# Count matrices from groups of 2 nodes with one tile of 128 edges each, and 18 instead of 16 dense blocks in attention 1

## The chip, the cores and the metric

The kernel runs on one core of one Trainium2 chip. The metric is the device time of one execution in microseconds. Of the core's engines, PE is the matrix engine (PEld its weight loads), DVE the vector engine, ACT the scalar engine, POOL the engine that issues the gathers here, and SP a queue for transfers.

## The reference

Two graph layers over 6250 nodes of 128 features and 200,000 edges (`src`, `dst`), which come sorted by `dst`. What matters here is the first, a graph attention in two layers, the first with 4 heads of 16 features and the second with one head:

```python
feat = (x @ W).reshape(num_nodes, H, D)
el = jnp.sum(feat * attn_l[None], axis=-1)
er = jnp.sum(feat * attn_r[None], axis=-1)
e = jax.nn.leaky_relu(el[src] + er[dst], NEG_SLOPE)
m = jax.ops.segment_max(e, dst, num_segments=num_nodes)
ee = jnp.exp(e - m[dst])
s = jax.ops.segment_sum(ee, dst, num_segments=num_nodes)
msg = feat[src] * (ee / s[dst])[:, :, None]
rst = jax.ops.segment_sum(msg, dst, num_segments=num_nodes)
```

The second graph layer is a convolution: a small network on each edge's attributes gives weights, the source node's row is gathered and combined with them, and the results are summed by `dst`.

## The kernel before

The nodes form 49 blocks of 128 (`NB`). The program has four stages, one after the other.

*Preparation.* `src` and `dst` are loaded and put into 16-bit integers (`raw`). The rows of x are normalised, multiplied by W1 and written to `table1`, 76 values a node. For counting, each group of W = 8 neighbouring destination nodes needs the place of its first edge in the sorted list: `belowc`, `wbelow` and `wseg` (L587 to L594) find the segment of 160 edges by comparing, seven gathers (L597) fetch those segments, and L601 to L608 make `wfirst` from them. A group starts anywhere, so its edges are read from the next lower multiple of WSTEP = 32, as a run of WCAP = 384 edges.

*Attention 1.* There are two ways to treat a block of destination nodes. An **edge block** (33 of them, `NG = NB - DENSE1`) goes over its up to 34 × 128 edges: POOL gathers a row of `table1` for each edge (L306, 34 indirect transfers a block, in groups of 8), DVE makes a one-hot matrix of destinations (`ohr`, L315) and the messages, PE sums them (`whole`, L362). The groups share 6 gather buffers `G`. A **dense block** (16, in pairs, `dense1`) uses no edges but a count matrix: how many edges go from each source node to each destination node. For 7 source blocks at a time and each head, ACT makes 7 `ramp` tiles (L833), DVE takes the minimum with the counts (`up`, L835), PE multiplies with `rc` (L847), a table of source rows that SP loads one step ahead. `ramp` and `up` have two buffers each. At a pair's end `finish1` writes its results.

The count matrices of all 49 blocks are made within attention 1 too, since attention 2 runs on them alone. `write_runs` writes `runs`, an array in device memory that has the 384 edges from each multiple of 32, during the first 4 edge blocks. `cut_windows` fetches the runs of 128 groups (16 groups are a block of nodes, so 7 such chunks), makes a `key` (source block × 8 + place in the group, with a large number added where the edge isn't of the group) and `lo` (place in the source block), and turns both with PE (`lot`, `keyt`). `count` then takes two groups: DVE compares `lot` with 0..127 (`lo`, L723) and `keyt` with 392 slots (`key`, L726), three tiles of 128 edges each; PE multiplies the two one-hot matrices, six matmuls of 392 columns (L731), three a group; ACT copies the sums to `ca` (L732), and ACT's queue writes a quarter of a block's counts to device memory (L922). Both comparisons read their constant side from a PSUM tile (`slots`).

The order of work is written in one loop over the edge blocks. After each group of gathers it adds count steps and dense steps in proportion, by two due counts: count steps from block LAG = 5, dense steps from block LAG_D = 8. From this program a scheduler makes the order within each engine; each engine then works in order.

*Attention 2* uses the count matrices for all 49 blocks, with the same sort of ramps and minima. *The convolution* gathers again, 34 transfers a block over all 49.

Of the kernel before, what the change touches and what calls it, by code (L numbers as in the profile page):

```python
# [26 lines left out]
F32 = mybir.dt.float32  # L27
# [11 lines left out]
P = 128  # L39
# [4 lines left out]
W, T = 8, 3  # L44
WCAP = P * T
WSEG = 160
WSTEP = 32
HS = 7
LAG = 5
AHEAD = 4  # L50
DENSE1, LAG_D = 16, 8
# [10 lines left out]
def gnn_kernel(ctx: ExitStack, tc: tile.TileContext, x, src, dst, attr4, attr8,  # L62
# [23 lines left out]
    assert WB % (2 * NQ) == 0  # L86
# [149 lines left out]
    raws = []  # L236
    for t in both:
        raw = pool.tile([P, ROWT + WCAP], BF16, tag="row", name="raw", bufs=2)[:GP].bitcast(I16)
        nc.scalar.copy(raw, t)
        raws.append(raw)  # L240
# [297 lines left out]
    slot_k = pool.tile([P, NKEY, 2], BF16, name="slot_k")  # L538
    nc.gpsimd.iota(slot_k, pattern=[[1, NKEY], [0, 2]], base=-(NKEY // 2), channel_multiplier=0,
# [9 lines left out]
    for b0 in range(0, NB, 4):  # L549
# [9 lines left out]
        for j in range(len(bs)):  # L559
# [18 lines left out]
    wstarts = find.tile([GP, NC * P], F32, name="wstarts")  # L578
    nc.gpsimd.iota(wstarts, pattern=[[W, NC * P]], base=0, channel_multiplier=0,
                   allow_small_or_imprecise_dtypes=True)  # L580
    NS = ROWT // WSEG
    wbelow = find.tile([GP, NC * P], F32, name="wbelow")
    ps = small()
    for c in range(NC):
        cs = slice(c * P, (c + 1) * P)
        below = find.tile([GP, P, NS], F32, name="belowc")
        nc.vector.tensor_tensor(below, df[:, 0:ROWT:WSEG][:, None, :].to_broadcast([GP, P, NS]),  # L587
                                wstarts[:, cs, None].to_broadcast([GP, P, NS]), op=OP.is_lt)
        nc.vector.tensor_reduce(wbelow[:, cs], below, axis=AX.X, op=OP.add)
        nc.tensor.matmul(ps[:, c:c + 1], wbelow[:, cs], ones[:GP], start=True, stop=True)  # L590
    wseg = find.tile([P, NC], F32, name="wseg")
    nc.vector.tensor_scalar(wseg, ps[:, :NC], -1.0, 0.0, op0=OP.add, op1=OP.max)
    wseg_i = find.tile([P, NC], I32, name="wseg_i")
    nc.vector.tensor_copy(wseg_i, wseg)  # L594
    wpart_i = find.tile([P, NC, WSEG], I32, name="wpart_i")
    for c in range(NC):
        nc.gpsimd.indirect_dma_start(  # L597
            out=wpart_i[:, c, :], out_offset=None, in_=dst.rearrange("(s t) -> s t", t=WSEG),
            in_offset=bass.IndirectOffsetOnAxis(ap=wseg_i[:, c:c + 1], axis=0))
    wpart = find.tile([P, NC, WSEG], F32, name="wpart")  # L600
    nc.vector.tensor_copy(wpart, wpart_i)  # L601
    nc.vector.tensor_tensor(wpart, wpart, own_w[:, :, None].to_broadcast([P, NC, WSEG]), op=OP.is_lt)
    wfound = find.tile([P, NC], F32, name="wfound")
    nc.vector.tensor_reduce(wfound, wpart, axis=AX.X, op=OP.add)
    nc.vector.scalar_tensor_tensor(wfound, wseg, float(WSEG), wfound, op0=OP.mult, op1=OP.add)
    nc.vector.tensor_scalar(wfound, wfound, float(E - WCAP), None, op0=OP.min)
    nc.vector.tensor_copy(wfirst, wfound)
    nc.vector.tensor_scalar(wfirst, wfirst, WSTEP.bit_length() - 1, None, op0=OP.logical_shift_right)  # L608

# [8 lines left out]
    nc.vector.tensor_copy(slots[:, :NKEY], slot_k.rearrange("p k j -> p (k j)").bitcast(F32))  # L618
    nc.vector.tensor_copy(slots[:, NKEY:NKEY + P // 2], slot_b.bitcast(F32))
    slot_k = slots[:, :NKEY].bitcast(BF16).rearrange("p (k j) -> p k j", j=2)  # L620
    slot = slots[:, NKEY:NKEY + P // 2].bitcast(BF16)
# [63 lines left out]
    def cut_windows(c):  # L685
        run = cut.tile([P, 2, WCAP], I16, name="run")
        nc.gpsimd.indirect_dma_start(
            out=run.rearrange("p j t -> p (j t)"), out_offset=None, in_=runs.rearrange("n j t -> n (j t)"),
            in_offset=bass.IndirectOffsetOnAxis(ap=wfirst[:, c:c + 1], axis=0))
        si, di = run[:, 0, :], run[:, 1, :]  # L690
# [4 lines left out]
        nc.vector.tensor_scalar(key, di, own_w[:, c:c + 1], -float(NKEY // 2), op0=OP.subtract, op1=OP.add)  # L695
        nc.vector.tensor_scalar(far, key, NKEY // 2 - (W - 1) / 2, None, op0=OP.add)
        nc.vector.tensor_tensor(far, far, far, op=OP.mult)
        nc.vector.tensor_scalar(far, far, -W * W / 4, 0.0, op0=OP.add, op1=OP.max)
# [4 lines left out]
        nc.vector.tensor_scalar(lo, hi, -float(P // 2), None, op0=OP.add)  # L703
        m = min(P, NSW - c * P)
        turned = []
        for name, v, copy in (("lot", lo, nc.vector.tensor_copy), ("keyt", key, nc.scalar.copy)):
            ps = quad()
            for j in range(T):
                nc.tensor.transpose(ps[:, j, :m], v[:m, j * P:(j + 1) * P], ident[:m, :m])
            t = cut.tile([P, T, P], BF16, name=name, bufs=2)  # L710
            copy(t[:, :, :m], ps[:, :T, :m])
            turned.append(t)
        return turned
# [4 lines left out]
    def count(b, quarter, ca, i):  # L718

        lot, keyt = tables[b * WB // P]  # L720
        sw = (b * WB + quarter * (WB // NQ) + i) % P
        lo = build.tile([P, T, P, 2], BF16, name="lo1")
# [5 lines left out]
        for k in range(2):  # L728
            ps = small()
            for j in range(T):  # L730
                nc.tensor.matmul(ps[:, :NKEY], lo[:, j, :, k], ky[:, j, :, k], start=j == 0, stop=j == T - 1)  # L731
            nc.scalar.copy(ca[:, :, (i + k) * W:(i + k + 1) * W], ps[:, :NKEY].rearrange("p (h d) -> p h d", d=W))  # L732
# [522 lines left out]
```

## Time and profile before

| | us |
|---|---|
| median of 3 runs | 4765.41 (4763.69 to 4770.68) |
| the profiled execution | 4768.61 |
| its span, first to last instruction | 4766.9 |
| attention 1: first gather to last `ramp` | 167 to 1958 |
| of it, from the first `lo` of counting | 438 |
| of it, from the first `ramp` of a dense block | 604 |
| last gather of attention 1 | 1899 |

Busy time is the time in which an engine ran instructions. A group line of the profile gives the line of the kernel, engine, operation, the tile written and the tile read with their shapes, the number of instructions, then busy time and mean length of one in ns, and after the second bar the engine's idle time just before them and what ended most of it.

### The profile page before, as it was taken

The page shows a single profiled execution, that of the slowest core. Times are in us where ns is not written, and L with a number is a line of the kernel's source. Part 1 is how long each engine was busy: PE and PEld are TensorE (multiplying, and loading weights), DVE is VectorE, ACT ScalarE, POOL GpSimd, SP SyncE. Part 2 cuts the span into 40 slices and gives each one's busy share as a digit, 9 for nine tenths or more (in the row PEclk, how much of TensorE's full clock was granted, in tenths as well). Part 3 has the DMA queues.
Part 4 walks back from the last instruction along what each step waited for, and adds up shares of the span by engine and source line. Part 5 has one row for each costly group of instructions (what it writes and reads, how often), then busy time and mean ns, then how long its engine had stood idle before and what let it go on. Part 6 is the DMA issues. An engine that isn't in the chain of part 4 may idle for free. (4 is left out here: it accounts for less than half of the span.)

```text
span 4766.9 us, 67078 instructions
## 1 busy us (share of the span) xinstructions
PE 3298.5 (69%) x22039; PEld 2390.4 (50%) x22040; DVE 3871.2 (81%) x6374; ACT 2921.4 (61%) x7165; POOL 2876.6 (60%) x2819
## 2 busy tenths in 40 slices
PE   1213677777677777499997767777777777777776
PEld 1212455555455455388885445445544545544544
DVE  5244999999899999588886888888888888888887
ACT  1121387787687787489996555555555555555554
POOL 0577776666666666100003777777777777777775
PEclk9999787888888888699997787788788878888787
DMA  3353455555455465544441222222222222222221
GB/s 83 85 129 86 129 151 151 153 153 146 141 149 150 138 168 146 167 141 170 143 160 57 55 58 57 56 57 58 56 58 57 56 57 58 59 57 57 58 56 42
DMA packets 318334, 478.01 MB, mean 100 GB/s; under 512 B 156389, under 2 KB 208147, under 8 KB 313738
## 3 DMA queue, kind: packets, MB, share of 16 engines
q1 hardware_dynamic: 177842, 226.64, 15.4%
q0 software_dynamic: 90032, 154.98, 14.2%
q10 hardware_dynamic: 50088, 91.88, 6.0%
q8 instruction: 179, 2.93, 0.3%
q14 instruction: 193, 1.58, 0.1%
HBM read 364.57 MB, written 108.67 MB: 99 GB/s over the span
## 5 line engine op out<-in xcount | busy, mean ns | idle before, releaser
L306 POOL DMA_INDIRECT G<-table,srcw x2788 | 2840.9, 1019 | 1611.9 <-issue 742.5
L1135 PE MATMUL whole<-halves,ohr 128*128 128x512 f32 x1666 | 625.3, 531 | 243.9 <-DVE halves L323 242.7
L731 PE MATMUL small<-key,lo 128*128 128x392 bf16 x2352 | 576.3, 380 | 202.6 <-DVE key L726 160.7
L833 ACT ACTIVATE ramp<-erb,sel 128x256 bf16<-128x256 f32 x1568 | 683.1, 501 | 2.5 <-DVE up L835 1.8
L1117 ACT ACTIVATE g<-G,a 128x128 f32<-128x128 f32 x1666 | 554.7, 395 | 143.6 <-DMA G<-table,srcw 133.8
L1135 PEld LDWEIGHTS whole<-halves,ohr 128*128 128x128 f32 x1666 | 409.8, 260 | 411.6 <-DVE halves L323 298.5
L726 DVE TENSOR_TENSOR key<-slots,keyt 128x2352 bf16<-128x2352 bf16 x392 | 537.0, 1370 | 0.1
L732 ACT CAST ca<-small 128x392 bf16<-128x392 f32 x784 | 368.4, 482 | 262.8 <-PE small L731 253.6
L1030 ACT ACTIVATE ramp<-small,sel 128x256 bf16<-128x256 f32 (+1 forms) x1225 | 447.6, 619 | 59.3 <-DVE up L1034 25.7
L323 DVE TENSOR_TENSOR halves<-mid,halves 128x1024 fp32r<-128x1024 f32 (+1 forms) x245 | 260.2, 1062 | 240.3 <-ACT halves L322 240.3
L731 PEld LDWEIGHTS <-lo 128*128 128x128 bf16 x2352 | 222.1, 108 | 421.2 <-DVE key L726 240.2
L1098 PE MATMUL small<-hid,wm_sb 128*128 128x512 f32 (+1 forms) x490 | 293.5, 685 | 141.2 <-ACT hid L1096 140.7
L1106 PEld LDWEIGHTS big<-wtp_sb,hid 64*128 64x128 f32 x3332 | 261.2, 218 | 257.8 <-ACT hid L1100 187.6
L1106 PE MATMUL big<-wtp_sb,hid 64*128 64x128 f32 x3332 | 323.5, 323 | 81.7 <-ACT hid L1100 81.7
L1100 ACT ACTIVATE hid<-small 128x512 f32<-128x512 f32 (+1 forms) x245 | 135.8, 554 | 368.0 <-PE small L1098 367.5
L1093 PE MATMUL small<-a8t,wm_sb 64*128 64x128 f32 (+1 forms) x1764 | 316.8, 322 | 41.5 <-ACT a8t L1088 41.5
L362 PE MATMUL whole<-halves,ohr 128*128 128x136 f32 x1122 | 208.4, 338 | 179.6 <-DVE halves L323 172.4
L1093 PEld LDWEIGHTS small<-a8t,wm_sb 64*128 64x128 f32 (+1 forms) x1764 | 266.2, 223 | 105.7 <-ACT a8t L1088 78.9
L1096 ACT ACTIVATE hid<-small 128x512 f32<-128x512 f32 (+1 forms) x245 | 134.0, 547 | 262.0 <-PE small L1093 262.0
L362 PEld LDWEIGHTS whole<-halves,ohr 128*128 128x128 f32 x1122 | 184.9, 244 | 199.3 <-DVE halves L323 145.9
L1039 PE MATMUL big<-rhs,up 128*128 128x196 bf16 x2401 | 240.5, 250 | 58.7 <-DVE up L1034 58.6
L847 PE MATMUL up<-rc,up 128*128 128x102 bf16 x3136 | 212.4, 225 | 75.8 <-DVE up L835 75.0
(277 smaller groups left out, 6217.6 us busy)
## 6 DMA issues: line engine op xcount, KB each, us to landing
counts<-ca ACTq DMA_DIRECT2D x196, 392.0 KB
ct<-counts SPq DMA_DIRECT2D x196, 392.0 KB
G<-table,srcw POOLq DMA_INDIRECT x2788
rc<-rhs SPq DMA_DIRECT2D x56, 717.5 KB
oht<-dlow SPq DMA_DIRECT2D x33, 1088.0 KB
ctc<-counts SPq DMA_DIRECT2D x448, 56.0 KB
a<-in_edge_attr SPq DMA_DIRECT2D x49, 136.0 KB
runs<-raw ACTq DMA_DIRECT2D x12, 450.0 KB
```

The costliest lines, as they stand in the source:

```text
L306: nc.gpsimd.indirect_dma_start(out=G[:, c, :], out_offset=None, in_=table, in_offset=bass.IndirectOffsetOnAxis(ap=idx[:, c:c + 1], axis=0))
L362: nc.tensor.matmul(acc, oh[:, c, :], ms[:, c].rearrange("e s f -> e (s f)"), start=start and c == 0, stop=stop and c == n - 1)
L726: nc.vector.tensor_tensor(ky, slot_k[:, None].to_broadcast([P, T, NKEY, 2]), keyt[:, :, None, sw:sw + 2].to_broadcast([P, T, NKEY, 2]), op ...
L731: nc.tensor.matmul(ps[:, :NKEY], lo[:, j, :, k], ky[:, j, :, k], start=j == 0, stop=j == T - 1)
L732: nc.scalar.copy(ca[:, :, (i + k) * W:(i + k + 1) * W], ps[:, :NKEY].rearrange("p (h d) -> p h d", d=W))
L833: nc.scalar.activation(ramp[:, i, :n * P], erb[:, h, :n * P], AF.Relu, bias=sel1[:, h0 + i, h:h + 1], scale=STEEP)
L1030: nc.scalar.activation(ramp[:, h, :n * P], pe[:, :n * P], AF.Relu, bias=sel2[:, h0 + h, :], scale=STEEP)
L1093: nc.tensor.matmul(ph[:, j * P:(j + 1) * P], wm1_sb[:n * NRAD, j, :], a8t[:n * NRAD, :], start=True, stop=True)
L1098: nc.tensor.matmul(ph[:, :npr * P], wm2_sb, hid1[:, :npr * P], start=True, stop=True)
L1106: nc.tensor.matmul(pw[:, c, :], hid2[half, j * P:(j + 1) * P], wtp_sb[half].rearrange("x p u -> x (p u)"), start=True, stop=True)
L1117: nc.scalar.activation(g0[:, c], G[:, c, :], AF.Copy, scale=a0[:, c, :])
L1135: nc.tensor.matmul(acc, oh[:, c, :], ms[:, c].rearrange("e s h i u -> e (s h i u)"), start=start and c == 0, stop=stop and c == n - 1)
```

## The change

Groups get 2 nodes instead of 8 (`W`), a run 128 edges instead of 384, from multiples of 16 instead of 32. There are 98 key slots instead of 392, 64 groups a block instead of 16, and 25 chunks of 128 groups instead of 7. A step of `count` takes a quarter of a block, 16 groups, in one comparison for `lo` and one for `key`; each group is one matmul of 98 columns, and four groups share a PSUM bank and one copy by ACT. The search for `wfirst` is split: its first half stays in the preparation, on 16-bit data, with 250 small matmuls; its second half (25 gathers and the comparisons) moves into the first edge blocks, two gathers after each group. `cut_windows` is split too: `fetch_run` fetches a run one chunk ahead. Dense blocks are 18 instead of 16, begun at edge block 7 instead of 8; 31 edge blocks are left.

In the order of the changed program POOL's 25 position gathers stand among the first 92 gathers of `G`, the first two runs after 194 gathers of `G`, and the other 23 runs one at a time from there on. On DVE two of the ten new comparisons `belowc` stand among the statistics of x, and eight after the first table; the 250 matmuls stand together on PE after the first table.

```diff
-W, T = 8, 3
-WCAP = P * T
+W = 2
+WCAP = 128
 WSEG = 160
-WSTEP = 32
+WSTEP = 16
-DENSE1, LAG_D = 16, 8
+DENSE1, LAG_D = 18, 7
...
-    wbelow = find.tile([GP, NC * P], F32, name="wbelow")
     ps = small()
-    for c in range(NC):
-        cs = slice(c * P, (c + 1) * P)
-        below = find.tile([GP, P, NS], F32, name="belowc")
-        nc.vector.tensor_tensor(below, df[:, 0:ROWT:WSEG][:, None, :].to_broadcast([GP, P, NS]),
-                                wstarts[:, cs, None].to_broadcast([GP, P, NS]), op=OP.is_lt)
-        nc.vector.tensor_reduce(wbelow[:, cs], below, axis=AX.X, op=OP.add)
-        nc.tensor.matmul(ps[:, c:c + 1], wbelow[:, cs], ones[:GP], start=True, stop=True)
+    for i in range(NS):
+        below = find.tile([GP, NC * P], BF16, name="belowc", bufs=2)
+        nc.vector.tensor_scalar(below, wstarts, df[:, i * WSEG:i * WSEG + 1], None, op0=OP.is_gt)
+        for c in range(NC):
+            nc.tensor.matmul(ps[:, c:c + 1], below[:, c * P:(c + 1) * P], ones_b, start=i + c == 0,
+                             stop=i == NS - 1 and c == NC - 1)
...
+    def seek_windows():
+        wfound = pool.tile([P, NC], F32, name="wfound")
+        for c in range(NC):
+            part = cut.tile([P, WSEG], I32, name="wpart_i", bufs=2)
+            nc.gpsimd.indirect_dma_start(
+                out=part, out_offset=None, in_=dst.rearrange("(s t) -> s t", t=WSEG),
+                in_offset=bass.IndirectOffsetOnAxis(ap=wseg_i[:, c:c + 1], axis=0))
+            yield
+            less = cut.tile([P, WSEG], F32, name="wpart")
+            nc.vector.tensor_scalar(less, part, own_w[:, c:c + 1], None, op0=OP.is_lt)
+            nc.vector.tensor_reduce(wfound[:, c:c + 1], less, axis=AX.X, op=OP.add)
...
+    def fetch_run(c):
+        run = cut.tile([P, 2, WCAP], I16, name="run", bufs=2)
+        nc.gpsimd.indirect_dma_start(
...
+        fetched[c] = run
...
-    def count(b, quarter, ca, i):
-        lot, keyt = tables[b * WB // P]
-        sw = (b * WB + quarter * (WB // NQ) + i) % P
-        lo = build.tile([P, T, P, 2], BF16, name="lo1")
...
-        for k in range(2):
-            ps = small()
-            for j in range(T):
-                nc.tensor.matmul(ps[:, :NKEY], lo[:, j, :, k], ky[:, j, :, k], start=j == 0, stop=j == T - 1)
-            nc.scalar.copy(ca[:, :, (i + k) * W:(i + k + 1) * W], ps[:, :NKEY].rearrange("p (h d) -> p h d", d=W))
+    def count(b, quarter, ca):
+        t = tables[b * WB // P]
+        sw = (b * WB + quarter * WQ) % P
+        lo, ky = [build.tile([P, WQ // 2, m, 2], BF16, name=name) for name, m in (("lo1", P), ("key1", NKEY))]
+        for j, (o, m) in enumerate(((lo, P), (ky, NKEY))):
+            shape = [P, WQ // 2, m, 2]
+            nc.vector.tensor_tensor(
+                o, slot_k[:, None, :m].to_broadcast(shape),
+                t[:, j, sw:sw + WQ].rearrange("p (a k) -> p a k", k=2)[:, :, None, :].to_broadcast(shape),
+                op=OP.is_equal)
+        for i in range(0, WQ, WBANK):
+            ps = small()
+            for k in range(WBANK):
+                a, r = divmod(i + k, 2)
+                nc.tensor.matmul(ps[:, k * NKEY:(k + 1) * NKEY], lo[:, a, :, r], ky[:, a, :, r],
+                                 start=True, stop=True)
+            nc.scalar.copy(ca[:, :, i * W:(i + WBANK) * W].rearrange("p h (k d) -> p h k d", d=W),
+                           ps[:, :WBANK * NKEY].rearrange("p (k h d) -> p h k d", k=WBANK, d=W))
...
+            if b < LAG - 1:
+                for _ in range(2):
+                    next(seeking, None)
...
+            if b == LAG - 1 and q == 3:
+                for c in chunks[:2]:
+                    fetch_run(c)
```

## The prediction

> **What bounds the kernel now.** I read the page's busy line and slices first, to find the stage; then busy time by stage; then the groups of that stage; then who waits for whom. Busy time over the whole span, and the slices, on the page:
>
> ```profile
> PE 3298.5 (69%) x22039; PEld 2390.4 (50%) x22040; DVE 3871.2 (81%) x6374; ACT 2921.4 (61%) x7165; POOL 2876.6 (60%) x2819
> ...
> DVE  5244999999899999588886888888888888888887
> ACT  1121387787687787489996555555555555555554
> POOL 0577776666666666100003777777777777777775
> ```
>
> A slice is 119 us. Slices 4 to 15 are attention 1, where counting starts: DVE shows 9 nearly throughout, ACT 7 to 8, POOL 6. All that the diff touches lies here and in the preparation; attention 2 and the convolution keep their code. Busy time by stage (window, length, then PE, PEld, DVE, ACT, POOL):
>
> ```profile
> 167.00:438.00 271.00, 60.27 (x382) 55.19 (x381) 111.76 (x261) 42.79 (x66) 205.81 (x204) 1.00 0.48 108
> 438.00:604.00 166.00, 106.58 (x551) 66.11 (x551) 136.44 (x231) 56.41 (x121) 116.91 (x120) 0.80 0.42 116
> 604.00:1958.00 1354.00, 985.80 (x7903) 695.40 (x7902) 1262.36 (x2090) 1044.62 (x2524) 865.17 (x807) 0.85 0.52 147
> ```
>
> 167 is the first gather, 438 the first comparison of counting (`lo`), 604 the first `ramp` of a dense block, 1958 the last one. In the long stage DVE is busy 1262/1354 = 93%, ACT 77%, PE 73%. Before 438, 204 gathers take 271 us, 1.33 us each: POOL, with the 0.30 us between two gathers, is full, and the others follow it. The groups:
>
> ```profile
> L306 POOL DMA_INDIRECT G<-table,srcw x2788 | 2840.9, 1019 | 1611.9 <-issue 742.5
> L731 PE MATMUL small<-key,lo 128*128 128x392 bf16 x2352 | 576.3, 380 | 202.6 <-DVE key L726 160.7
> L833 ACT ACTIVATE ramp<-erb,sel 128x256 bf16<-128x256 f32 x1568 | 683.1, 501 | 2.5 <-DVE up L835 1.8
> L726 DVE TENSOR_TENSOR key<-slots,keyt 128x2352 bf16<-128x2352 bf16 x392 | 537.0, 1370 | 0.1
> L732 ACT CAST ca<-small 128x392 bf16<-128x392 f32 x784 | 368.4, 482 | 262.8 <-PE small L731 253.6
> ```
>
> and the same view by form, within 438 to 1962:
>
> ```profile
> L835 DVE TENSOR_TENSOR up<-ramp,ctc 128x1792 bf16<-128x1792 bf16 x224 | 241.5, 1082 | 20.1 <-ACT ramp L833 19.1
> L723 DVE TENSOR_TENSOR lo<-slots,lot 128x768 bf16<-128x768 bf16 x392 | 214.3, 547 | 22.6 <-PE small L731 22.4
> ```
>
> The two comparisons, `key` and `lo`, are 751 of DVE's 1402 us between 438 and 1962. Idle time in the same window, by releaser (total, times, longest):
>
> ```profile
> ACT ca L732 <- PE small L731: 253.6, 284, 7.6
> POOL G L306 <- DVE msg L355: 170.5, 31, 12.3
> ```
>
> ACT idles for PE, PE for `key`, POOL for DVE to free a gather buffer: every chain of waits ends at DVE.
>
> [...] from 768 to 2352 elements the time grows 547 to 1370 ns, 0.520 ns an element, and the 1792 of L835 lie on the line (0.520 × 1792 + 148 = 1080; shown 1082). [...] 10 ramps of 501 ns took 4.10 us. [...] 14 pairs of 102 columns in 0.82 us, and I use the trace:
>
> ```profile
> 1308.17 4.10 ACT L833 ACTIVATE ramp<-erb,sel 128x256 bf16<-128x256 f32 x10
> ...
> 1308.62 1.21 PE L731 MATMUL small<-key,lo 128*128 128x392 bf16 x6 [0.70 <-DVE key L726]
> ...
> 1310.75 0.82 PE L847 MATMUL up<-rc,up 128*128 128x102 bf16 x14 [0.92 <-DVE up L835]
> ```
>
> **The change, part by part.**
>
> *Counting, DVE.* Before: 392 × (547 + 1370) ns = 751 us. After: 49 × 4 = 196 quarters, each with a `lo` of 8×128×2 = 2048 elements (148 + 0.520 × 2048 = 1213 ns) and a `key` of 8×98×2 = 1568 (963 ns): 196 × 2.176 = 427 us. [...] Gain 325 us.
>
> *Counting, PE and ACT.* PE: 392 × 1.21 = 474 us become 196 × 16 pairs; by the 14 in 0.82, about 0.92 us a quarter, 180 us. ACT: still 784 casts of 392 columns, 368 us; no gain.
>
> *Dense blocks, 16 to 18.* One more pair costs ACT an eighth of 683 = 85 us of ramps and some 6 of copies; DVE 28 × 1.08 = 30 and some 15 at its end; PE some 36; SP's queue 7 more loads of `rc` and 56 of `ctc`. Two edge blocks go: 68 gathers × 1.33 = 90 us of POOL, 2 × 17 us of DVE, 2 × 3 of ACT.
>
> *Cutting, 7 chunks to 25.* DVE 7 × 4.2 = 30 us become 25 × some 2 = 50. The run is fetched a chunk ahead, so the 18.6 us that `hi` (L692) waited for it should go; POOL pays 18 more gathers.
>
> DVE from 438 on: 1402 − 325 + 45 + 20 − 34 = 1108. Over the stage length found below that is 81%: DVE no longer bounds. What is late next is ACT.
>
> *Preparation.* DVE spends 26 us (55 to 77) on `belowc` and `wbelow`, ahead of the statistics on which table 1 hangs. In the order of the changed program two of ten new comparisons stand there (about 1.1 us each, if they run like `oht`, 4352 elements in 1371 ns); eight follow after, with 250 one-column matmuls at some 80 ns (the `pe` matmuls L348 run 8 in 0.67): 20 us, where the old chain took 20 from `wseg` to `wfirst`, DVE waiting 16 of them for seven landings. I take the first gather 20 us earlier (0 to 25): 147.
>
> *Blocks 0 to 4.* POOL gets 25 position gathers and two of runs here: 27 × 1.33 = 36 us. A position gather waits until DVE has used the one two before it, with the `G` gathers queued behind it on POOL; a landing takes 7 us (last issue 154.1, compare 161.4), mostly under other gathers; I add 10 (0 to 40). `runs` gets 25,000 rows of 256 bytes for 12,500 of 768: fewer bytes, twice the packets, written under POOL's time; nothing on the path, priced below as a rival. Counting starts at 438 − 20 + 46 = 464.
>
> *Blocks without dense work.* Two instead of three, now at POOL's pace: 70 × 1.33 = 93 us, dense work from 557 (before 604).
>
> *The long stage.* ACT: 1045 + 91 (pair) + 32 casts more within it (724 for 692, 15 us) + 5 (`turned`) − 3 (one block) = 1153 us. How full can ACT be? In attention 2, where the same ramps feed the same kind of work, it is:
>
> ```profile
> 2040.00:2160.00 120.00, 108.52 (x1146) 100.97 (x1144) 101.17 (x175) 107.55 (x293) 0.00 (x0) 0.97 0.45 158
> 2160.00:2280.00 120.00, 111.31 (x1203) 103.52 (x1201) 105.03 (x194) 113.08 (x314) 0.00 (x0) 1.00 0.44 152
> 2280.00:2400.00 120.00, 108.06 (x1138) 100.22 (x1136) 101.21 (x188) 106.98 (x295) 0.00 (x0) 0.99 0.44 159
> ```
>
> 327.6/360 = 91%; DVE as the bound here reached 93%. I take 91%: 1153/0.91 = 1267, last ramp at 1824 instead of 1958, **134 us less**. POOL allows it: 1104 gathers × 1.33 from 147 end at 1615, and before, the stage ended 62 us after its last gather (1900 to 1962): 1677.
>
> The profiled execution took 4768.6 us (span 4766.9 and 1.7 around it), 3.2 above the median of three, 4765.4. 4768.6 − 134 = 4634.6; less 3.2, about 4632.
>
> **The rivals.**
>
> *A: ACT's waits stay* (slower). ACT idled 1354 − 1045 = 309 us here, mostly casts behind PE, and a quarter still sends four banks of sums through the same two PSUM buffers, on an engine that works in order. If that idle stays, the stage lasts 1153 + 309 = 1462 and ends at 2019: +61, 4826. It decides from an idle time of 1958 − 557 − 1153 = 248 us (ACT 82% full). Against it: PE waited for `key`, which now gets much shorter. [...]
>
> *B: the small writes.* The second hardware queue (q10) took 6.0% of 16 engines for 50,088 packets: 91 ns each. 12,500 more are 71 us on all 16. Blocks 0 to 4 have room (DMA 48%), but if gathers land late by all of it, the gain is 63: 4703.
>
> *C: ACT nearly full.* At 97% the stage takes 1189 and the gain is 212: 4554.
>
> *D: counts fall out of the 128-edge window* and blocks are redone. In the inputs the fullest group of two nodes has 101 edges; with at most 15 lost to the step of 16 that is 116. Excluded.
>
> **How the numbers follow.** Forecast (ACT 87 to 95% full) 0.55, B or a share of 83 to 86% 0.16, C 0.14, A 0.11, a tie 0.04. A measurement can tell about 0.2%, 9.5 us. Faster 0.85, same 0.04, slower 0.11. C's middle is the low end, 4555; the high end, 4748, is a share of 84% (1373 us, gain 28) with about 10 us lost early; that leaves out A and half of C.
>
> **What would show it.** Right: `key` near 0.96 and `lo` near 1.21 us, 196 each; DVE near 80% and ACT over 87% between first and last ramp; the first ramp near 557, the last near 1824. Wrong: ACT idle for PE above 248 us there (A); the first ramp after 600 (B, or stalls of the position gathers)[...].

## The result, and the profile after

| | before | after |
|---|---|---|
| median, us | 4764.48 (4751.04 to 4773.15, 10 runs) | 4741.39 (4729.82 to 4751.44, 10 runs) |
| ratio | 1 | 0.9955, 95% interval 0.994 to 0.997 |
| profiled execution; its span, us | 4768.61; 4766.9 | 4744.26; 4742.4 |
| first gather | 167.0 | 138.6 |
| first `ramp` of a dense block | 604.6 | 515.1 |
| last `ramp` of a dense block | 1958.0 | 1930.1 |

The change is faster by 23 us (the interval is 14 to 29); the forecast, 4632, was 132 us below the kernel before. The table shows where the rest went: dense work begins 89 us earlier, and 62 of these are given back before it ends. The long stage lasts 1415 us (before 1354).

Busy time on the page of the changed kernel, with the slices of PE, DVE and ACT and the TensorE clock:

```profile
PE 3194.4 (67%) x23441; PEld 2530.2 (53%) x23442; DVE 3624.8 (76%) x6107; ACT 2981.9 (63%) x7370; POOL 2855.6 (60%) x2787
...
PE   3124576766666666489896777777777777777776
...
DVE  4256687777777877488886888888888888888887
ACT  2012578777878787589895555555555555555555
...
PEclk9999766667667766699997788888787887888788
```

In slices 4 to 15 DVE fell from 9 to mostly 7 or 8, and ACT did not rise: nothing took DVE's place as a full engine. The same stage as a window (length, then PE, PEld, DVE, ACT, POOL busy, the clock, DMA share, GB/s):

```profile
515.00:1931.00 1416.00, 930.43 (x9175) 850.21 (x9176) 1092.93 (x1908) 1123.61 (x2768) 888.30 (x823) 0.67 0.51 148
```

ACT is 1123.6/1416 = 79% busy, DVE 77%, PE 66%. ACT's idle time, 292 us, is almost what it was in the kernel before (309), although the work from which the forecast traced that idle time, DVE's `key`, has shrunk. The groups, from the view by line; two of them are the new comparisons:

```profile
L845 ACT ACTIVATE ramp<-erb,sel 128x256 bf16<-128x256 f32 x1764 | 758.0, 501 | 16.9 <-DVE up L847 12.5 <-DMA counts<-ca 2.0 <-DMA ctc<-counts 1.7
L743 ACT CAST ca<-small 128x392 bf16<-128x392 f32 x784 | 348.7, 484 | 183.8 <-PE small L741 168.2 <-DMA counts<-ca 8.0 <-issue 1.7
L741 PE MATMUL small<-key,lo 128*128 128x98 bf16 x3136 | 322.2, 248 | 140.0 <-ACT ca L743 124.2 <-DVE key L733 7.5 <-ACT turned L719 3.1
L859 PE MATMUL up<-rc,up 128*128 128x102 bf16 x3528 | 318.3, 264 | 216.6 <-DVE up L847 212.4 <-DVE rr L777 3.2 <-issue 0.2
L733 DVE TENSOR_TENSOR lo<-slots,turned 128x2048 bf16<-128x2048 bf16 x196 | 239.4, 1222 | 121.5 <-PE small L741 118.9 <-PE pe L350 1.6
L733 DVE TENSOR_TENSOR key<-slots,turned 128x1568 bf16<-128x1568 bf16 x196 | 189.2, 965 | 0.0
```

The comparisons take 239 + 189 = 429 us, as worked out. But each of the three engines now waits for another in a ring. Waits within the long stage (total, times, longest):

```profile
ACT ca L743 <- PE small L741: 147.8, 151, 9.7
...
DVE lo L733 <- PE small L741: 118.2, 95, 5.5
DVE up L847 <- ACT ramp L845: 87.1, 82, 3.4
...
PE up L859 <- DVE up L847: 212.4, 116, 10.4
PE small L741 <- ACT ca L743: 114.9, 138, 3.2
```

ACT waits for PE, PE for ACT and DVE, DVE for PE and ACT. PE's longest waits in the long stage of the kernel before:

```profile
PE small L731 <- DVE key L726: 131.8, 167, 2.8
PE up L847 <- DVE up L835: 75.0, 80, 2.9
PE every L841 <- DMA rc<-rhs: 60.0, 26, 7.3
PE small L731 <- ACT ca L732: 33.2, 45, 2.7
```

Its wait for `key` is down to 2.5 us, but its wait for `up` rose from 75 to 212 us and its wait for ACT's casts from 33 to 115.

One figure is new: the clock of TensorE is 0.67 in this stage, and was 0.85. The clock records of this trace show only two levels, 1 and 0.5, 205 records of each, in lengths that are multiples of 3.41 us (the one at the trace's end aside). What moves it between the two they do not show; that it is PE's lighter load which takes the clock away is tested below (w3). (The clock of 1.00 in the prediction's first window, with PE 22% busy, is no reading: the clock records of that trace begin at 465 us.) The matmuls of the dense blocks became longer on average, 225 ns in the kernel before (the line below) and 264 in the changed one:

```profile
L847 PE MATMUL up<-rc,up 128*128 128x102 bf16 x3122 | 211.6, 225 | 75.8 <-DVE up L835 75.0
```

From the timeline of the changed kernel:

```profile
1200.23 0.86 PE L741 MATMUL small<-key,lo 128*128 128x98 bf16 x8 [0.66 <-ACT ca L743]
...
1201.00 1.37 PE L859 MATMUL up<-rc,up 128*128 128x102 bf16 x14
```

Here 14 pairs of 102 columns take 1.37 us where the prediction's excerpt has 0.82.

### The profile page after: what moved, and what is told of

It reads as the page before. It is cut to its first block, busy times and chain, and to the rows that moved or that the text cites. A ratio compares the mean times of both kernels' runs of the same rounds, so it can differ in the third digit from the quotient of the medians.

```text
span 4742.4 us, 69914 instructions
## 1 busy us (share of the span) xinstructions
PE 3194.4 (67%) x23441; PEld 2530.2 (53%) x23442; DVE 3624.8 (76%) x6107; ACT 2981.9 (63%) x7370; POOL 2855.6 (60%) x2787
## 5 line engine op out<-in xcount | busy, mean ns | idle before, releaser
L308 POOL DMA_INDIRECT G<-table,srcw x2720 | 2784.9, 1024 | 1638.5 <-issue 715.4
L845 ACT ACTIVATE ramp<-erb,sel 128x256 bf16<-128x256 f32 x1764 | 758.0, 501 | 16.9 <-DVE up L847 12.5
L1156 PEld LDWEIGHTS whole<-halves,ohr 128*128 128x128 f32 x1666 | 410.3, 260 | 411.1 <-DVE halves L325 297.4
L859 PE MATMUL up<-rc,up 128*128 128x102 bf16 x3528 | 318.3, 264 | 216.6 <-DVE up L847 212.4
L741 PE MATMUL small<-key,lo 128*128 128x98 bf16 x3136 | 322.2, 248 | 140.0 <-ACT ca L743 124.2
L859 PEld LDWEIGHTS <-up 128*128 128x128 bf16 x3528 | 268.1, 129 | 245.0 <-DVE up L847 238.3
L364 PE MATMUL whole<-halves,ohr 128*128 128x136 f32 x1054 | 239.5, 386 | 201.8 <-DVE halves L325 186.1
L1121 ACT ACTIVATE hid<-small 128x512 f32<-128x512 f32 (+1 forms) x245 | 135.8, 554 | 368.4 <-PE small L1119 367.9
L847 DVE TENSOR_TENSOR up<-ramp,ctc 128x1792 bf16<-128x1792 bf16 x252 | 274.0, 1088 | 105.4 <-ACT ramp L845 87.1
L733 DVE TENSOR_TENSOR lo<-slots,turned 128x2048 bf16<-128x2048 bf16 x196 | 239.4, 1222 | 121.5 <-PE small L741 118.9
L364 PEld LDWEIGHTS whole<-halves,ohr 128*128 128x128 f32 x1054 | 214.2, 294 | 209.0 <-DVE halves L325 145.3
```

The costliest lines, as they stand in the source:

```text
L308: nc.gpsimd.indirect_dma_start(out=G[:, c, :], out_offset=None, in_=table, in_offset=bass.IndirectOffsetOnAxis(ap=idx[:, c:c + 1], axis=0))
L364: nc.tensor.matmul(acc, oh[:, c, :], ms[:, c].rearrange("e s f -> e (s f)"), start=start and c == 0, stop=stop and c == n - 1)
L741: nc.tensor.matmul(ps[:, k * NKEY:(k + 1) * NKEY], lo[:, a, :, r], ky[:, a, :, r], start=True, stop=True)
L845: nc.scalar.activation(ramp[:, i, :n * P], erb[:, h, :n * P], AF.Relu, bias=sel1[:, h0 + i, h:h + 1], scale=STEEP)
L859: nc.tensor.matmul(ups[k][:, h], up[:, i, k * P:(k + 1) * P], by_head[:, i, :, h, :], start=h0 + i + h == 0, stop=h0 + i + h == NB + H1 - 2)
L1156: nc.tensor.matmul(acc, oh[:, c, :], ms[:, c].rearrange("e s h i u -> e (s h i u)"), start=start and c == 0, stop=stop and c == n - 1)
```

## The experiments

All ratios are against runs of the kernel before on the same chip; the changed kernel is at 0.9955. "Stage" is from the first `ramp` of a dense block to the last, in one profiled execution of each kernel. Executions of the changed kernel lie up to 22 us apart, so differences of 10 us between stages, or of 0.2% between ratios, say little. A half step is one group of 7 ramps with their minimum and the 14 matmuls behind it: 28 to a pair of dense blocks, 252 for 18 blocks and 224 for 16 (the expectations also say "dense step").

| kernel | stage, us | ACT busy / idle in it | ratio (95%) |
|---|---|---|---|
| before | 1354 | 1045 / 309 | 1 |
| changed | 1416 | 1124 / 292 | 0.9955 (0.994 to 0.997) |
| w1: 16 dense blocks, lag 8 | 1335 | 1030 / 305 | 0.9890 (0.9873 to 0.9906) |
| x10: 16 dense blocks, lag 7 | 1389 | 1050 / 339 | 0.9898 (0.9875 to 0.9922) |
| w3: more matmuls | 1451 | 1139 / 312 | 1.0040 (1.0015 to 1.0065) |
| w4: half count steps | 1428 | 1122 / 306 | 1.0006 (0.9997 to 1.0015) |
| w5: loads two ahead | 1409 | 1124 / 285 | 0.9949 (0.9932 to 0.9965) |
| x6: a cast of four on DVE | 1406 | 1057 / 349 | 0.9943 (0.9922 to 0.9964) |
| x8: matmuls a half step later | 1426 | 1124 / 302 | 0.9969 (0.9957 to 0.9981) |
| y12: banks between ramps | 1454 | 1123 / 331 | 1.0014 (1.0004 to 1.0023) |
| y14: three buffers | 1432 | 1124 / 308 | 0.9975 (0.9965 to 0.9985) |
| z17: no points between pairs | 1392 | 1127 / 265 | 0.9885 (0.9869 to 0.9902) |
| z19: z17 and x6 | 1362 | 1057 / 305 | 0.9855 (0.9834 to 0.9875) |
| x7: x6 and 16 blocks, lag 8 | 1315 | 968 / 347 | 0.9873 (0.9853 to 0.9893) |
| y15: y12, y14 and 16 blocks, lag 8 | 1358 | 1035 / 323 | 0.9935 (0.9910 to 0.9961) |
| z18: z17, x6 and 16 blocks, lag 8 | 1258 | 967 / 291 | 0.9742 (0.9726 to 0.9758) |

### The parts of the change: counting alone (w1, x10)

```diff
-DENSE1, LAG_D = 18, 7
+DENSE1, LAG_D = 16, 8
```

> The changed kernel with 16 blocks dense ahead and 8 kept, as the kernel before has: 224 dense steps in place of 252, two blocks more with edges. If a dense step costs what the stage's length over its steps says, 5.6 us, and an edge block's gathers are covered, 28 steps fewer are -157 us in attention 1, and the two blocks more at 34 gathers of 1.33 us are +90: about 4675. If the stage is bound by gathers (59 us per block), +118 and nothing back: about 4840. Clock: fewer dense steps, TensorE still less busy, clock 0.65 to 0.70.

> The changed kernel with 16 dense blocks, begun after 7 blocks as in the changed kernel: 224 dense steps spread over 27 blocks from about 515 us. If the gain of 16 blocks over 18 (4715 against 4742) is 28 steps saved at 5 to 6 us each less two blocks of gathers, an earlier begin gives back part of the 61 us by which the first ramp came later: about 4670 to 4700. If the long stage is held by its blocks with edges and not by the dense steps, 4705 to 4725.

Measured: 4714.95 us and 4711.18 us. The new counting alone brings 0.9890, and the two dense blocks more, with the lag of 7, bring it back to 0.9955: they cost 0.65%, about 31 us. At the same lag of 7 (x10) it is 0.57%. Neither price that was offered for w1 held. The 28 half steps fewer shortened the stage by 81 us, but it also began 61 us later, and the two blocks more with edges are in it. An earlier begin (x10) moves the first `ramp` from 576 to 516 and leaves the end where it was: 1911 and 1905. Its time lies in the range of "held by its blocks with edges and not by the dense steps" (4705 to 4725). The stage of w1 as a window:

```profile
576.00:1911.00 1335.00, 887.97 (x8600) 811.79 (x8600) 1046.69 (x1853) 1030.09 (x2540) 902.26 (x841) 0.65 0.53 150
```

Against the kernel before, with as many dense steps, DVE lost 216 us of work here and the stage 19; another 28 us come before it, as the first `ramp` is at 576.4 instead of 604.6. ACT's idle time is 305 us.

### The clock (w3)

```diff
         for i in range(0, WQ, WBANK):
             ps = small()
+            for a in range(2):
+                nc.tensor.matmul(ps[:, :4 * NKEY], lo[:, i // 2 + a, :, 0],
+                                 ky[:, i // 2:i // 2 + 2].rearrange("p a m k -> p (a m k)"), start=True, stop=True)
```

> The changed kernel with two more matmuls of 392 columns in each bank of the counts, written over by the four real ones: about 0.3 us more of TensorE per bank, 784 banks, some 240 us. This kernel was looked at once on a chip where its convolution is bound differently; this is the comparison on a chip like that of the times before. Clock: granted clock in the long stage at 0.80 or over (changed kernel 0.67), the 102-column matmul near 230 ns (264), time -40 to +10 us against the changed kernel's 4741. Banks: each bank comes 0.3 us later, time +40 to +150 us. Loads: no change of the waits on rc, time +0 to +60 us.

Measured: 4796.34 us. The window and the group:

```profile
536.00:1987.00 1451.00, 1082.85 (x10608) 886.27 (x10606) 1086.58 (x1892) 1138.90 (x2767) 865.68 (x807) 0.81 0.51 145
```
```profile
L862 PE MATMUL up<-rc,up 128*128 128x102 bf16 x3528 | 277.6, 242 | 179.1 <-DVE up L850 175.2 <-DVE rr L780 3.3
```

More work on PE (1083 us or 75% of the stage, for 930 or 66%) does bring the clock back, 0.67 to 0.81, and the matmuls of the dense blocks from 264 to 242 ns; so it is PE's lighter load that let the clock fall. But the time goes up by 0.85%, and ACT's idle time with it, 292 to 312 us. The 55 us more lie in the ranges of the theories of the banks and of the loads. That the slower clock costs something is not excluded, since the added matmuls cost time themselves; that it is what keeps the forecast's gain away is not supported by this run.

### Banks, loads and the place of the matmuls (w4, w5, x8)

```diff
# w4: a quarter's comparisons and first two banks at one due point, its last two banks at the next
-    steps = [(b, quarter) for b in order for quarter in range(NQ)]
+    steps = [(b, quarter, part) for b in order for quarter in range(NQ) for part in range(2)]
# w5: rc and ctc with bufs=3
-                    ahead = load(b0, n, h0 + HS)
+                    ahead.append(load(b0, n, h0 + 2 * HS))
# x8: the matmuls of a half step in a function that is called in the next one
+                    if late is not None:
+                        late()
+                    late = lambda up=up, by_head=by_head, h0=h0, h=h: weigh(up, by_head, h0, h)
```

> The changed kernel with the four banks of a quarter split into two due points. Banks: VectorE's wait for the sums before lo falls from 118 us to below 60, ScalarE's before the casts from 148 to below 80, time about -50 us against 4741. Clock: the clock stays at 0.67 and the 102-column matmul at 264 ns, waits move from the casts to the ramps, time within 15 us. Loads: waits on rc unchanged, time within 15 us.

> The changed kernel with three buffers for rc and for the counts of a dense step, loaded two steps ahead. Loads: TensorE's wait for rc falls from 65 us to below 20, ScalarE's idle time with it, time about -40 us against 4741. Banks and clock: the wait for rc goes, the waits for sums and for up grow by the same, time within 15 us.

> The changed kernel with the 14 matmuls of a half step written one half step later, so that TensorE does not come to them before VectorE's minimum is done. In-order loop: TensorE's wait for up falls from 212 us to below 60, and with it ScalarE's wait for the banks behind those matmuls from 148 to below 90; time 4640 to 4690. ACT plus idle: TensorE's wait goes, ScalarE's idle time stays at about 300 us, time within 15 us of 4741.

Measured: 4772.46, 4740.48 and 4746.52 us. None of the three edits made the kernel faster. In w4 DVE's wait before `lo` rose to 167 us, presumably because a comparison's buffers are held over two due points. In w5 PE's wait for `rc` stays, 64.1 us: the trace shows, at most steps, the matmuls of `every` (sums that need `rc` and the counts but no ramp) 4 to 8 us after the issue of their `rc`, as in the changed kernel, while the ramps of that step begin some 29 us after `every` (in the changed kernel 10). So the earlier load is met by an earlier `every`, and the wait moves with it. In x8 PE's wait for `up` rose, 212 to 236 us: writing these matmuls later did not bring PE to them later than the minimum. (A step's loads are issued one half step later in x8 too; PE's wait for `rc` stays, 65 us.) In none of the three did the wait shrink at which the edit was aimed, so they show that these edits do not help, and not that those waits cost nothing.

### ACT's work (x6, x7)

```diff
-            nc.scalar.copy(ca[:, :, i * W:(i + WBANK) * W].rearrange("p h (k d) -> p h k d", d=W),
+            copy = nc.vector.tensor_copy if i == WBANK else nc.scalar.copy
+            copy(ca[:, :, i * W:(i + WBANK) * W].rearrange("p h (k d) -> p h k d", d=W),
```

> The changed kernel with one of the four casts of a quarter on VectorE in place of ScalarE: ScalarE's busy time in the long stage falls by 196 x 0.48 = 94 us, VectorE's rises by about as much or a little more, to about 85%. Theory ACT plus idle: the stage lasts ScalarE's work plus about 300 us of its idle time, whatever else is done (309, 292, 305, 312, 306 and 285 us in the runs so far), so it gets about 90 us shorter: about 4655. Theory of the in-order loop (ramp, minimum, matmul, bank of sums, cast, each in the order written, none of the three engines full): half of that at most, as VectorE's copies now stand in its own queue ahead of the next minimum: about 4700 to 4745.

> One of four casts on VectorE, and 16 dense blocks with a lag of 8. ACT plus idle: about 4715 - 85 = 4630. In-order loop: 4675 to 4715.

Measured: 4735.48 and 4700.60 us. The long stage of x6:

```profile
522.00:1928.00 1406.00, 955.29 (x9188) 867.44 (x9188) 1161.44 (x2084) 1056.78 (x2589) 878.69 (x818) 0.66 0.52 149
```

ACT lost 67 us of work in it, and the stage 10, no more than executions differ; ACT's idle time rose to 349. With 16 blocks the figures are 62 and 20. So the stage does not last ACT's work and a fixed idle time, although ACT is the busiest engine of the changed kernel: "its work and about 300 us" was a coincidence of the earlier kernels. The copies went to DVE, which has 69 us more work and is 83% busy here; that they took back a part of what ACT won is not excluded. Both times lie in the range of the in-order loop, whose own test, x8, did not bear it out: that theory stays open.

### The order of the banks, and buffers (y12, y14, y15)

```diff
# y12: count() only queues its four banks
+        banks.extend(partial(one_bank, i) for i in range(0, WQ, WBANK))
# y12: and dense1 takes one after every second ramp
+                        if i % 2 and banks:
+                            banks.popleft()()
# y14
-    build = one.enter_context(tc.tile_pool(name="build", bufs=2))
+    build = one.enter_context(tc.tile_pool(name="build", bufs=3))
```

> The changed kernel with the banks of a quarter (four matmuls and their cast) no longer in one row after its two comparisons, but one after every second ramp of the dense half steps that follow, with the same work in all. Theory of the written order (ScalarE stands at a bank that TensorE is still filling, VectorE then waits for the ramps behind it, TensorE for the minimum): ScalarE's wait for the banks falls from 148 us to below 60, VectorE's for the ramps from 87 to below 60, time 4640 to 4700. Theory of the two buffers of lo and key: the comparison of the quarter after next still waits for the last bank of this one, 118 us or more, time within 15 us of 4741, or longer. If neither sets the stage: waits move, time within 15 us.

> The changed kernel with three buffers in place of two for lo, key and the block's counts. Theory of the two buffers: VectorE's wait for the banks before lo falls from 118 us to below 40, and the minimum, the weights of the edges and the gathers behind it come earlier, time 4640 to 4700. Theory of the written order: the wait for lo goes, ScalarE's for the banks stays at about 148 us, time within 15 us of 4741.

> 16 dense blocks with a lag of 8, three buffers for lo, key and the counts, and the banks between the ramps. With 16 blocks alone it was 0.9890 of the kernel before, 4715. If the order and the buffers each free their waits: 4600 to 4660. If only one of the two counts: 4640 to 4690. If neither sets the stage: 4700 to 4730.

Measured: 4774.00, 4755.65 and 4740.79 us: none faster than the same kernel without the edit (0.9955 for the first two, 0.9890 for the third). In y12 the waits did shift as the order says, and their sum did not fall:

```profile
ACT ca L746 <- PE small L744: 184.7, 119, 22.5
...
DVE lo L736 <- PE small L744: 190.1, 118, 6.2
...
DVE up L856 <- ACT ramp L852: 34.1, 40, 2.4
```

DVE's wait for the ramps fell from 87 to 34 us, its wait for the banks rose from 118 to 190. A third buffer (y14) took the latter only to 99. Neither this order nor a third buffer shortens the stage.

### The stretches between two pairs (z17, z18, z19)

The dense blocks come in nine pairs of 196 ramps. Two pairs and what lies between them as windows of the changed kernel (868 to 991 is the third pair but for its last 3 us, 991 to 1019 the time until the fourth, and so on):

```profile
868.00:991.00 123.00, 84.28 (x887) 77.59 (x886) 99.90 (x151) 113.18 (x278) 82.06 (x77) 0.65 0.55 163
991.00:1019.00 28.00, 19.90 (x159) 18.20 (x160) 23.97 (x63) 14.15 (x38) 21.78 (x21) 0.75 0.59 167
1019.00:1155.00 136.00, 86.20 (x890) 79.04 (x888) 103.38 (x168) 113.86 (x282) 84.54 (x77) 0.69 0.51 147
1155.00:1182.00 27.00, 19.48 (x147) 17.79 (x145) 23.15 (x59) 12.03 (x32) 19.99 (x20) 0.63 0.58 160
```

ACT is 92% busy in the third pair, 84% in the fourth and 45 to 51% between. ACT's timeline between the third and the fourth:

```profile
997.69 0.65 ACT L324 CAST halves<-msg 128x544 fp32r<-128x544 f32 x1
...
1005.25 0.31 ACT L753 ACTIVATE e<-e 128x128 f32<-128x128 f32 x1 [6.91 <-DVE e L752]
1006.51 0.65 ACT L324 CAST halves<-msg 128x544 fp32r<-128x544 f32 x1 [0.95 <-DVE msg L357]
...
1016.80 0.59 ACT L829 COPY erb<-bank 128x512 f32<-128x512 f32 x1 [1.78 <-PE bank L827]
1018.51 0.59 ACT L829 COPY erb<-bank 128x512 f32<-128x512 f32 x1 [1.12 <-PE bank L827]
1018.99 2.91 ACT L845 ACTIVATE ramp<-erb,sel 128x256 bf16<-128x256 f32 x7
```

A pair's end (DVE's sums and `finish1`, L752 and L753) and the next one's `erb`, which has one buffer, stand between the last ramp and the next first one. Taken strictly from the last ramp of a pair to the first of the next, there are eight such stretches, 168 us together, with ACT 38% busy; inside the pairs ACT is 85% busy (1247 us). For the kernel before the same two figures are 31% in 189 us and 85% in 1165 us.

```diff
+        nxt = load(NG, min(2, NB - NG), 0), spread(NG, min(2, NB - NG))
...
+                elif b0 + 2 < NB:
+                    nxt = load(b0 + 2, min(2, NB - b0 - 2), 0), spread(b0 + 2, min(2, NB - b0 - 2))
...
-            yield
...
-    n_dense = -(-DENSE1 // 2) * (2 + H1 * (NB // HS))
+    n_dense = -(-DENSE1 // 2) * (H1 * (NB // HS))
```

(`spread` makes `erb`, now with two buffers; both `yield` lines at a pair's begin and end go.)

> The changed kernel with no due point of its own for a pair's begin and end: erb and the first loads of the next pair are written at the last step of the pair before, with two buffers for erb, and the 252 half steps alone are spread over the edge blocks (270 points before). In the changed kernel ScalarE is 85% busy inside the nine pairs (1247 us) and 38% in the eight stretches between them (168 us, 21 each). Theory of the gaps: the stretches shrink from 21 us to below 10, the stage by 60 to 100 us: 4640 to 4690. Rival (work that now stands between the pairs, edge blocks and counting, moves inside and displaces ramps there): stretches shorter, pairs longer, ScalarE below 82% inside, time within 15 us of 4742.

> The same on 16 dense blocks with a lag of 8, and with one of the four casts of a quarter on VectorE; with the casts alone it was 0.9873 of the kernel before. Theory of the gaps: seven stretches of 23 us shrink to below 10, 0.970 to 0.980. Rival: 0.985 to 0.990.

> 18 dense blocks with a lag of 7, no points for a pair's begin and end, and one of four casts on VectorE. In the changed kernel the casts moved alone took 10 us from the long stage and the points alone 24. If the two are separate costs, together 30 to 40 us: stage about 1380, 4700. If each of them hid the other (a ScalarE free inside the pairs has no ramps to make between them, and gaps closed only displace ramps while it is full inside), more than their sum: stage 1310 to 1350, about 4630 to 4670.

Measured: 4711.24, 4645.79 and 4695.38 us. The long stage of z17:

```profile
515.00:1907.00 1392.00, 914.70 (x9185) 837.36 (x9185) 1090.51 (x1909) 1127.27 (x2773) 876.98 (x823) 0.68 0.53 151
```

In z17 the stretches shrank from 168 us to 11, and the stage by 24: inside the pairs ACT fell from 85% to 81%, as work displaced from the stretches came in. (The edit also changed the order at the begin: most position gathers run ahead of the first gather, which comes at 161.7; the first `ramp` stays at 515.) So both sides had a part right; the time gained, 0.70% or 33 us, is past what the rival allowed and short of the theory. In z19 casts and stretches together bring 1.00% (0.9955 to 0.9855), where they bring 0.12% and 0.70% alone. That is more than the sum by less than the intervals; the stage lost 54 us where the sum is 34. The time, 4695, is near that of separate costs, the stage, 1362, lies between the two forecasts.

z18 puts them on 16 dense blocks and is the best kernel here, 2.6% under the kernel before and 2.1% under the changed one; its 0.9742 lies in the range of the theory of the gaps. Blocks, casts and stretches bring 0.65%, 0.12% and 0.70% alone, 1.47% in sum, and 2.1% together: a part of what each is worth shows only with the others. Its long stage, and some of the waits in it:

```profile
577.00:1835.00 1258.00, 879.75 (x8617) 794.96 (x8616) 1099.88 (x2029) 967.25 (x2371) 921.82 (x843) 0.66 0.57 160
```
```profile
POOL G L308 <- issue: 219.5, 720, 0.3
ACT ca L744 <- PE small L741: 203.2, 155, 16.7
...
POOL G L308 <- DVE msg L357: 24.9, 13, 4.6
...
DVE lo L733 <- PE small L741: 21.4, 17, 3.0
```

Here an engine is near full again: POOL's gathers with the 0.3 us between two of them are (922 + 220)/1258 = 91% of the stage, DVE is at 87%, and DVE's wait for the banks is down from 118 to 21 us. ACT's wait for the banks is longer than in the changed kernel, 203 us for 148, in a stage that is 158 us shorter. Against z19 the two dense blocks fewer are worth 1.1%.

### Another chip

The kernels of w1, w3, w4 and w5 were also run on a chip on which the kernel before took 6176.92 us. What they were expected to do there was:

> The changed kernel with 16 dense blocks and dense work from block 8, as before: the new groups alone. Two views of the long stage (first to last ramp, 1416 us in the changed kernel). If a dense step is what costs, 1416/252 = 5.6 us each whatever stands between, 224 of them take some 1260 us, the first ramp comes one block later (some 565), and the kernel is some 50 to 100 us faster than with 18 dense blocks (4650 to 4690). If an edge block is what costs, 59 us each, 25 of them take 1475, and the kernel is some 100 us slower (4840). The prediction's sum (ACT full to 91%) has 1062/0.91 = 1167 us. Clock theory (PE has less work[...]): granted clock in the long stage at 0.67 or below.

> The changed kernel with two idle matmuls of 392 columns ahead of each bank's four of 98; their sums are overwritten. PE streams 1176 columns a bank, as before the change, and gets 1568 x 0.18 = some 280 us of work at full clock more. Clock theory (PE has so little work that its clock is granted at 0.67 instead of 0.85, which lengthens every PE stretch that others wait for): the clock of the long stage goes back to 0.80 or more, the mean of the 102-column matmuls from 264 to some 230 ns, and the kernel is no slower, -40 to +10 us. Bank theory (four banks of sums pass two PSUM buffers on engines that work in order) and load theory (rc lands too late): the clock may rise, but PE holds each bank longer, and the kernel is 30 to 150 us slower.

> The changed kernel with the same work in another order: of a quarter's four banks two are made right after the comparisons and two at the next due point, so that two banks at a time meet two PSUM buffers, as before the change. Bank theory: DVE's wait of lo for PE falls from 118 to below 60 us, ACT's wait of ca for PE from 148 to below 80, PE's for ca from 115 to below 50, and the kernel is 50 us or more faster. Clock theory and load theory: within 15 us of the changed kernel, clock still near 0.67.

> The changed kernel with three buffers instead of two for rc and ctc, and their loads two steps of seven source blocks ahead instead of one. Load theory (in the long stage PE stands 65 us for rc and 15 for counts, up to 6.5 at a time, with count matmuls and sums queued behind): this wait falls below 20 us and the kernel is 40 us or more faster. Clock theory: the wait falls, PE is idle elsewhere instead, and the kernel is within 20 us of the changed one; a part of the gain may come where the clock rises by 0.03 or more. Bank theory: within 15 us.

Measured: 6227.70, 6265.40, 6195.50 and 6164.26 us, ratios 1.0100 (1.0071 to 1.0129), 1.0109 (1.0027 to 1.019), 1.0018 (0.9984 to 1.0052) and 0.9973 (0.9945 to 1.000). The changed kernel was not run there, so they say little of it. A stretch of the convolution, 3000 to 4000, on that chip and on the other for the kernel with 16 dense blocks:

```profile
3000.00:4000.00 1000.00, 602.76 (x3437) 436.43 (x3435) 612.89 (x977) 465.25 (x1180) 475.15 (x487) 0.73 0.19 53
```
```profile
3000.00:4000.00 1000.00, 736.15 (x3609) 497.66 (x3605) 827.74 (x1216) 570.15 (x1375) 765.95 (x769) 0.81 0.23 57
```

POOL's instructions, nearly all of them gathers, are 0.98 us long on the first and 1.00 on the second, but only 487 of its instructions come in the time of 769. What holds them apart was not found. There the kernel with more blocks with edges (1.0100) does worse than those with 18 dense blocks (1.0018 and 0.9973), the other way round than above.

## Why the prediction was right and wrong

**Right: what was removed.** `key` 965 ns and `lo` 1222 ns, 196 each, 429 us (427 forecast; that the 0.520 ns an element of the comparisons before would hold for the new shapes was an estimate); DVE is no longer full (77% of the long stage); no trouble from the small writes: the first `ramp` is not late.

**Mis-sized, to the better: the early part.** First gather 138.6 (forecast 147), first `lo` 441.5 (464), first `ramp` 515.1 (557). The 10 us for stalls of the position gathers were not needed, as 225 POOL instructions took 302 us, 1.34 each; and 58 instead of 70 of them lie between the first `lo` and the first `ramp`.

**The step that failed: "I take 91%".** ACT's work was about right, 1124 us (1153 forecast). But it fills 79% of the stage, which is 1415 us and not 1267. Attention 2, from which the 91% came, has no gathers, no counting and no blocks with edges among its ramps. The fit figure stood in the kernel before: ACT is 85% busy inside the pairs there, with DVE at 94%, and 85% in the changed kernel, with DVE at 76%. Easing DVE did not raise it. Of the 292 us of idle time, some 105 lie between the pairs (168 × 0.62) and 187 inside. The sentence before it failed as well: "What is late next is ACT". In x6 ACT lost 67 us of work and the stage 10, so a sum of ACT's work over a fill could not give the length of this stage. And "every chain of waits ends at DVE" was read from too few waits: before the change PE also stood 60 us for `rc` and 33 for ACT's casts.

**Next to it: PE's work was mis-sized.** The counting matmuls were sized from 14 pairs in 0.82 us, 180 us in all; they are busy 322, at the lower clock (0.67 in the long stage, for 0.85) and in groups of four with gaps between; how much each of the two adds was not separated.

**Rival A came nearest.** It said that ACT's idle time stays, and where: casts behind PE, through two PSUM buffers (147.8 of the 292 us). It was laid aside because PE's wait for `key` would go; it went, and PE's waits for ACT (33 to 115 us) and for `up` (75 to 212) came in its place. The result is still on the faster side because the other terms moved: with the first `ramp` at 515.1 and 1124 us of work, A's deciding idle time is 1958 − 515 − 1124 = 319 us, not 248. But A's reason was not borne out. It, too, took ACT's work and idle time for the length of the stage, against which x6 speaks; and in z18 the wait behind the banks is longer and the stage shorter.

**Luck.** The time, 4741, lies just inside the stated range, under its high end of 4748. That end stood for ACT 84% full in a stage of 1373 us. The stage took 1415 at 79%, and only a begin that was 42 us earlier than forecast (515 for 557) made up for it.

**What the forecast held and did not draw out.** By its own numbers the pair of dense blocks adds 91 us to the engine that it made the bound, and takes 90 us from POOL, whose own sum would have ended the stage at 1677, 147 us ahead of ACT's. Leaving the pair out (w1) gains 31 us. The earlier begin of dense work, at block 7 instead of 8, is worth nothing with 16 blocks (x10).

**Slips without weight.** The 26 us of `belowc` and `wbelow` lie at 45 to 77, not 55 to 77; the 0.67 us of eight `pe` matmuls is that of their weight loads, the matmuls took 0.59; 4634.6 less 3.2 is 4631.4.

**Open.** The two edits that gained without touching the number of blocks, casts and stretches, take 54 of the stage's 1416 us together. What keeps ACT idle for the rest inside the pairs was not found. Finer banks, other order, a third buffer, later matmuls, earlier loads and a higher granted clock (0.81 for 0.67), each tried by itself (w3, w4, w5, x8, y12, y14), did not help; but most of these edits left standing the wait at which they were aimed. The waits go round in the ring of PE, ACT and DVE, and an edit at one place moved them to another. Not tried: in the changed kernel POOL's gathers wait 148 us for DVE (by the view for `w`, L352), up to 14 us at a time, so they hang on this ring too.

## What to carry to other kernels

When the full engine is relieved, do not take the fill of another stage for the next one; read the fill of the second engine in this very stage, split where its work breaks off (here between pairs), and do not count on its idle time to go. An edit that trades work from one engine to another (dense for edge blocks) has to be priced anew when the bound moves: it was the smaller number of blocks, together with two small edits, that brought the stage to 1258 us. A wait at the top of the list is not a cause until taking it away shortens the stage: ACT's longest wait grew from 148 to 203 us in the best kernel.

## What the runs showed of the hardware

In the long stage PE's busy time fell from 986 us of 1354 to 930 of 1416, and with it the granted clock from 0.85 to 0.67; two further matmuls a bank (1083 us busy of 1451) brought it back to 0.81. So in this stage a lighter load on PE made its matmuls longer: 102 columns took 225, 264 and 242 ns on average in the three. Each engine worked in a fixed order where this can be read: behind attention 1, where the program is the same, 4371 instructions of ACT, 3513 of DVE, 1676 of POOL and 12,984 matmuls of PE come in the same order in the traces before and after. And two chips ran the kernel before in 4764 and 6177 us; in the kernel with 16 dense blocks POOL's instructions were of nearly the same length on both (0.98 and 1.00 us in a stretch of the convolution), but further apart on the slower one.
